# A two-pass graph network kernel: attention worked out by products inside pass 2, late edges scattered at the end, and pass 2's rows gathered as three bf16 parts

## The chip, the core and the metric

The kernel runs on one core of a Trainium2 chip. The metric is the device time of one execution in microseconds (us), the median of several runs. Beside it stands one profiled execution with a trace; the durations quoted come from that one.

## What is computed

There are 12500 nodes with 256 features each and 200000 edges (src, dst), sorted by dst. The reference is, cut to what matters:

```python
h = relu(layernorm(x))
h = h @ W_pre + b_pre
h = relu(gcn_conv(h, W1, b1)); h = relu(gcn_conv(h, W2, b2))   # with self loops, norm by degrees
x = x + h @ W_post + b_post
h = relu(layernorm(x))
xt = (h @ weight).reshape(N, 4, 64)
alpha = softmax(leaky_relu(alpha_l[src] + alpha_r[dst]), over the 4 heads)   # one row per edge
tmp[n] = sum over heads of alpha[n] * xt[dst[n]]        # n counts edges: edge n writes node n
x = x + tmp, repeated for the 4 heads
```

`alpha_l` and `alpha_r` are products of `xt` with small vectors, 4 numbers per node. The attention thus uses edges 0 to 12499 alone, edge n for node n. As the edges are sorted by dst, the dst of these lie in the first nine tiles of 128 nodes (XW = 9), while their src lie anywhere.

## The kernel before, in words

Nodes come in NT = 98 tiles of 128, edges in NCH = 112 chunks of 14 groups of 128 (the last chunk has 9 groups). The helper `convolve` (L1153) runs one convolution over all edges; it is called twice, as pass 1 and pass 2, with a table of rows in DRAM.

For each group t, POOL issues an indirect DMA (L1374) that gathers the 128 source rows into `fgot`, a ring of four buffers of one chunk each in pass 2. VectorE makes the one-hot matrices `fhot` of a whole chunk at once (L1241), and TensorE multiplies one-hot by rows into the sum `facc` in PSUM (L1382), which an fp32 matmul does in two records of the trace. At a chunk's end `close` lets ScalarE copy the sum (`fsums`, L1276), TensorE turn it (`fturn`, L1206, eight groups later) and VectorE add it to a sliding window `buf` (L1293, 13 groups later).

When a tile's window is complete, the steps of `finish1` (L1410) or `finish2` (L1464) are put into the list `due`, each with an offset in groups: `at` enters a step, `run` does all that are due, and `fills` names the PSUM tile that a step fills, so that a step that takes it over comes first. These offsets set the order of instructions on each engine; each engine runs its instructions in that order.

- `finish1`: product with W2's predecessor (L1417, +6), then ScalarE's relu into `fo` (L1422, +10), written to `table2` on the ACT queue.
- `finish2`: product with W2 (`fpz` L1472, +6), relu (`fy` L1479, `fz` L1482, +8), W_post (`fpo` L1488, +12), residual `fx` and its statistics, `kept_x` written on SP's queue (L1493 to L1501, +14), `h` on ScalarE (L1509, +16), its transpose (`fpt` L1514, +20; `ht` L1518, +22), the attention products (`fpx` L1527, +26), and at +28 a copy and small writes of `alpha_l` to `table_l` and `table_e` (L1535), of the first nine tiles' rows to `table_r`.

`prepare2` (L1454) loads what the next tile needs on SP's queue. Pass 2's first chunk is gathered by its own lists (`lacking`), so that it needs no row of pass 1's last two tiles; `late_sums` adds these by one-hots.

After pass 2 comes the attention stage (L1605 to L1711): for each group of seven tiles, POOL gathers `alpha_l[src]` per edge (`fal`, L1662); the rows of dst are built by one-hots `hot_t` (L1572) and products `fends` (L1652) out of `rows` (gathered by `own_rows`, L1577); products `lacks` (L1633) fill in src tiles that were not there at an earlier gather; VectorE does the softmax and the weighted sums `near`, `far`, `some`, `more`, `fmix`, `fres` (L1666 to L1694), and SP stores the group's 896 KB. The rows of 14 tiles are made inside pass 2 (L1553, for tiles 40 to 53).

If a check of the edge list fails, `bad_row` sends the execution to a general path, which is not part of the times here.

Of the kernel before, what the change touches and what calls it, by code (L numbers as in the profile page):

```python
# [413 lines left out]
def fast_path(  # L414
# [57 lines left out]
    table2 = dram.tile([NT * P, D], F32, name="ftable2")  # L472
    kept_x = dram.tile([NT * P, D], F32, name="kept_x")
# [3 lines left out]
    assert AC * J == NT and AC * CE <= E and XW < NT  # L477
    table_r = dram.tile([XW * P, DR], F32, name="table_r")
    table_l = dram.tile([NT * P, H], F32, name="table_l")

    LW = 3
    table_e = dram.tile([NT * P, H], F32, name="table_e")
# [18 lines left out]
    base_b = const.tile([P, NCH], F32, name="base_b")  # L501
    row_i = const.tile([P, AC], I32, name="row_i")
# [88 lines left out]
    with tc.tile_pool(name="fprep", bufs=1) as prep:  # L591
# [233 lines left out]
        with tc.tile_pool(name="fpsum", bufs=2, space=PSUM) as psum, \  # L825
# [227 lines left out]
            wide = prep.tile([NCH, P], F32, name="wide")  # L1053
            nc.vector.tensor_copy(wide, base.to_broadcast([NCH, P]))
# [7 lines left out]
            nc.tensor.matmul(fk[:, 2, :NCH], wide, ident[:NCH, :NCH], start=True, stop=True)  # L1062
# [7 lines left out]
            for f in after:  # L1070
                f()
            after = [raw_block(ends, m, psum.tile([P, 4 * P], F32, name="ft"), j0)
                     for j0 in (8, 12)]
            nc.vector.tensor_copy(base_b, fk[:, 2, :NCH])
            nc.vector.tensor_scalar(row_i, base_b[:, :AC], lane, float(XW * P - 1), op0=ALU.add,
                                    op1=ALU.min)
# [16 lines left out]
    def check_chunks(work, psum):  # L1093
# [20 lines left out]
        kept = work.tile([1, 1], F32, name="n_kept", bufs=1)  # L1114
        nc.vector.tensor_reduce(kept, pt[:1, 2, :NCH], AX.X, ALU.add)
        nc.vector.tensor_add(kept, kept, counted)
        nc.vector.tensor_scalar(bad_row, kept, -1.0, float(NCH + 1), op0=ALU.mult, op1=ALU.add)
# [12 lines left out]
    def load_late(pool):  # L1130

        nc.scalar.dma_start(roots, root_t)
        for t, w in ((wb, w2), (wo, w_post), (wg[:, :, :D], w_gat)):
            nc.scalar.dma_start(t, w.rearrange("(k p) n -> p k n", p=P))
        nc.scalar.dma_start(b2c, b2.rearrange("(k p) -> p k", p=P))
        nc.scalar.dma_start(bob, b_post.partition_broadcast(P))
        attn = []
        for a in (attn_r, attn_l):
            ar = pool.tile([P, D], F32, name="far", bufs=2)
            nc.scalar.dma_start(ar, a.rearrange("h c -> (h c)").partition_broadcast(P))  # L1140
            attn.append(ar)
        return attn

    def late_weights(pool, attn):

        for i, ar in enumerate(attn):
            for k in range(KC):
                prod = pool.tile([P, H, C], F32, name="fprod", bufs=1)
                nc.vector.tensor_mul(prod.rearrange("p h c -> p (h c)"), wg[:, k, :D], ar)
                nc.vector.tensor_reduce(wg[:, k, D + i * H:D + (i + 1) * H], prod, AX.X,  # L1150
                                        ALU.add)

    def convolve(ep, table, stride, width, ahead, with_sum, psum, prepare, finish, lacking=False,  # L1153
                 raw=(), rows_p=None):
# [28 lines left out]
        def run(now=None):  # L1183

            while due:
# [3 lines left out]
                do(d)  # L1189

# [41 lines left out]
        const_p = psum.tile([P, P if with_sum else P + D], F32, name="iota_p", bufs=1)  # L1232
        iota_p = const_p[:, :P]
        nc.vector.tensor_copy(iota_p, iota_w)
        if not with_sum:
            state["bias"] = const_p[:, P:]
            nc.vector.tensor_copy(state["bias"], bob)

# [4 lines left out]

        def hot_of(c):

            n = nj[c]
            h = ep.tile([P, J, P], F32, name="fhot", bufs=3)
# [3 lines left out]
        def new_rows_of():  # L1251
            if with_sum:
                return new_got()
            return rows_p.tile([P, J, stride], F32, name="fgot", bufs=ahead)

        def late_sums():

            h = ep.tile([P, J, P], F32, name="fhot", bufs=3)
# [5 lines left out]
            px = psum.tile([P, KC, P], F32, name="fpt", bufs=1)  # L1264
# [100 lines left out]
        for t, (c, j) in enumerate(tiles):  # L1365
# [7 lines left out]
            if c >= len(raw):  # L1373
                nc.gpsimd.indirect_dma_start(  # L1374
                    out=got, out_offset=None, in_=table[:(NT - TW) * P, :] if some else table[:],
# [4 lines left out]
            if j == (5 if some else 2) and c + 1 < NCH:  # L1380
                hots[c + 1] = hot_of(c + 1)
            nc.tensor.matmul(acc, hots[c][:, j, :], got[:, :width], start=(j == 0),  # L1382
                             stop=(j == nj[c] - 1 and not some))
# [6 lines left out]
            if c + 1 < len(raw):  # L1390
                raw_ahead(c + 1, j)
            run(t)
        run()
# [16 lines left out]
    def finish1(work, psum, w, buf, sbuf, fs):  # L1410
# [9 lines left out]
        def e():  # L1420
            o = work.tile([P, D], F32, name="fo", bufs=3)
            nc.scalar.activation(o, v["po"], AF.Relu, scale=dinv2[:, w:w + 1])  # L1422
            nc.scalar.dma_start(table2[w * P:(w + 1) * P, :], o)
            if w == 8:
                late_weights(late, attn)
                first_chunk()
            if w == 9:
                check_chunks(late, psum)

        return [(6, d, fills(w, "fpo")), (10, e, None)]  # L1430

    with tc.tile_pool(name="psum1", bufs=1, space=PSUM) as psum, \
# [6 lines left out]
                 rows_p=late)  # L1439
    ring.close()  # L1440

    ap = ctx.enter_context(tc.tile_pool(name="fatt", bufs=2))
    rows = [ap.tile([P, DR], F32, name="rows", bufs=AC) for c in range(AC)]
    EARLY = 2

    FROM = 40
    assert J % G == 0 and FROM > XW + 2 and FROM + J < NT - LW
    lates = {w: ap.tile([P, DA], F32, name="fxl", bufs=LW) for w in range(NT - LW, NT)}
    early = [ap.tile([P, G, DR], F32, name="fxe", bufs=J // G) for g in range(J // G)]
    hot_l = [ap.tile([P, CE], F32, name="hot_l", bufs=LW) for i in range(LW)]  # L1450

    def prepare2(work, w):  # L1454
# [6 lines left out]
        nc.sync.dma_start(xb[:n, :], x[w * P:w * P + n, :])  # L1461
        return rb, xb

    def finish2(work, psum, w, buf, pre, bias):  # L1464
        v = {"root": pre[0], "x": pre[1]}

        def d():
            pz = in_psum(psum, w, "fpz", [P, D], "facc", [P, D], 2)
# [16 lines left out]
        def f():  # L1485
            po = v["po"] = in_psum(psum, w, "fpo", [P, D], "facc", [P, D], 2)
# [4 lines left out]
        def g():  # L1491
# [9 lines left out]
            nc.scalar.activation(v["sc"], mv[:, 1:2], AF.Sqrt, bias=eps)  # L1501

# [8 lines left out]
        def i():  # L1511
            pt = v["pt2"] = in_psum(psum, w, "fpt", [P, KC, P], "fturn", [P, 2 * KC, P])
            for k in range(KC):
                nc.tensor.transpose(pt[:, k, :], v["h"][:, k * P:(k + 1) * P], ident)  # L1514

        def k():
            v["ht"] = work.tile([P, KC, P], F32, name="ht2")
            nc.scalar.activation(v["ht"], v["pt2"][:, :KC, :], AF.Copy)  # L1518
# [4 lines left out]
        def q():  # L1523
            px = in_psum(psum, w, "fpx", [P, DA], "iota_p", [P, P + D])
            px = v["px"] = px[:, d0:] if w + 1 < NT else px[:, :H]
# [4 lines left out]
        def r():  # L1530
            if w < NT - LW:
                xa = work.tile([P, DA], F32, name="fxa")
            else:
                xa = lates[w]
            nc.scalar.activation(xa[:, d0:], v["px"], AF.Copy)  # L1535
            nc.scalar.dma_start(table_l[w * P:(w + 1) * P, :], xa[:, DR:])
            if w < NT - LW:
                nc.scalar.dma_start(table_e[w * P:(w + 1) * P, :], xa[:, DR:])
            if w < XW:
                nc.scalar.dma_start(table_r[w * P:(w + 1) * P, :], xa[:, :DR])  # L1540

        steps = [(6, d, fills(w, "fpz")), (8, e, None), (12, f, fills(w, "fpo")), (14, g, None),
                 (16, h, None), (20, i, fills(w, "fpt")), (22, k, None),
                 (26, q, fills(w, "fpx")), (28, r, None)]
        t = w - FROM
        if 0 <= t < J:

            if t == 0:
                own_rows(0)

            def ends():
                px = v["ends"] = in_psum(psum, w, "fpx", [P, DA], None, None)[:, :DR]
                nc.tensor.matmul(px, hot_t[0][:, t * P:(t + 1) * P], rows[0], start=True,  # L1553
                                 stop=True)

            def copied():
                nc.scalar.activation(early[t // G][:, t % G, :], v["ends"], AF.Copy)

            steps += [(32, ends, "fpx"), (34, copied, None)]
        return steps  # L1560


    hot_t = {}

    def load_ends(pool, c, bufs):
        to_all = pool.tile([P, CE], I32, name="to_all", bufs=bufs)
        nc.sync.dma_start(to_all, dst[c * CE:(c + 1) * CE].partition_broadcast(P))
        return to_all

    def turn_hots(pool, c, to_all, bufs):  # L1570
        hot_t[c] = pool.tile([P, CE], F32, name="hot_t", bufs=bufs)
        nc.vector.tensor_scalar(hot_t[c], to_all, base_b[:, c:c + 1], lane,  # L1572
                                op0=ALU.subtract, op1=ALU.is_equal)

    def own_rows(c):

        nc.gpsimd.indirect_dma_start(  # L1577
            out=rows[c], out_offset=None, in_=table_r[:],
            in_offset=bass.IndirectOffsetOnAxis(ap=row_i[:, c:c + 1], axis=0))

    with tc.tile_pool(name="psum2", bufs=1, space=PSUM) as psum, \
            tc.tile_pool(name="fwork2", bufs=2) as work, \
            tc.tile_pool(name="edges2", bufs=1) as ep, \
            tc.tile_pool(name="fgots2", bufs=1) as rows_p:
        ep.tile([P, 320], F32, name="apart")
        for c in range(EARLY):
            turn_hots(ap, c, load_ends(work, c, 1), EARLY)
# [165 lines left out]
```

## Time and profile before

| | before |
|---|---|
| median of 9 runs | 4920.44 us (4892.04 to 4943.21) |
| the profiled execution | 4897.55 us |
| its span in the trace | 4895.7 us |
| granted TensorE clock, mean | 0.722 |
| pass 2, first to last gather issued | 2345.76 to 4634.98 us |
| last `fpx` | 4684.49 us |

How to read the views. In a line of the page's fifth part stand line, engine, operation, written tile and read tiles, how often, busy time in us, mean of one in ns, and the engine's idle time just before with what ended it. "issue" is time in which the engine waited for nothing that the profile shows; "remote" is a release by something that the profile does not name. A timeline line has start and length in us and, in brackets, the idle time before. Windows give each engine's busy time in a stretch of the span.

```profile
core 0: us, PE busy (x) PEld busy (x) DVE busy (x) ACT busy (x) POOL busy (x), PEclk, DMA share, GB/s
1000.00:1500.00 500.00, 287.57 (x978) 199.79 (x976) 79.59 (x138) 25.24 (x58) 330.84 (x351) 0.71 0.38 105
3000.00:3500.00 500.00, 267.33 (x1161) 226.52 (x1162) 112.55 (x240) 51.22 (x138) 319.46 (x338) 0.75 0.41 108
4640.00:4690.00 50.00, 34.32 (x169) 27.43 (x170) 18.96 (x60) 13.01 (x36) 5.45 (x6) 0.88 0.19 54
4690.00:4896.00 206.00, 82.27 (x245) 51.20 (x244) 107.96 (x202) 33.98 (x97) 91.48 (x96) 0.61 0.46 146
```

The four stretches lie in pass 1, in pass 2, at its end and in the attention stage.

### The profile page before, as it was taken

The page shows a single profiled execution, that of the slowest core. Times are in us where ns is not written, and L with a number is a line of the kernel's source. Part 1 is how long each engine was busy: PE and PEld are TensorE (multiplying, and loading weights), DVE is VectorE, ACT ScalarE, POOL GpSimd, SP SyncE. Part 2 cuts the span into 40 slices and gives each one's busy share as a digit, 9 for nine tenths or more (in the row PEclk, how much of TensorE's full clock was granted, in tenths as well). Part 3 has the DMA queues.
Part 4 walks back from the last instruction along what each step waited for, and adds up shares of the span by engine and source line. Part 5 has one row for each costly group of instructions (what it writes and reads, how often), then busy time and mean ns, then how long its engine had stood idle before and what let it go on. Part 6 is the DMA issues. An engine that isn't in the chain of part 4 may idle for free. (4 is left out here: it accounts for less than half of the span.)

```text
span 4895.7 us, 32267 instructions
## 1 busy us (share of the span) xinstructions
PE 2703.4 (55%) x10600; PEld 2070.1 (42%) x10600; DVE 1139.7 (23%) x2421; ACT 487.1 (10%) x1233; POOL 3103.0 (63%) x3299
## 2 busy tenths in 40 slices
PE   5655555555655655556445555454555555455553
PEld 4534433334434433434334444444444444444441
DVE  7412111111111111111222221222222222222236
ACT  5200000000000000000001110010111001100111
POOL 7566666666666666665566666666666666666633
PEclk7766767777766766676777777777777777777766
DMA  9433333333333333333334443443444444444434
GB/s 280 132 105 104 104 104 106 104 104 106 105 104 105 104 106 105 103 105 94 118 104 112 112 115 106 112 108 107 111 109 112 110 111 114 107 108 106 108 106 157
DMA packets 327419, 554.57 MB, mean 113 GB/s; under 512 B 96301, under 2 KB 224836, under 8 KB 327244
## 3 DMA queue, kind: packets, MB, share of 16 engines
q0 software_dynamic: 153520, 414.16, 31.4%
q1 hardware_dynamic: 127878, 121.99, 8.2%
q10 hardware_dynamic: 45846, 16.27, 1.3%
q8 instruction: 87, 1.43, 0.1%
q14 instruction: 88, 0.72, 0.0%
HBM read 498.89 MB, written 53.21 MB: 113 GB/s over the span
## 5 line engine op out<-in xcount | busy, mean ns | idle before, releaser
L1374 POOL DMA_INDIRECT fgot<-ftable,fsrc_t x3056 | 2892.0, 946 | 1564.6 <-issue 900.6
L1382 PE MATMUL facc<-fgot,fhot 128*128 128x257 f32 (+1 forms) x6252 | 1863.2, 439 | 625.5 <-issue 584.9
L1382 PEld LDWEIGHTS facc<-fgot,fhot 128*128 128x128 f32 x6252 | 1346.1, 223 | 981.4 <-issue 763.2
L1293 DVE TENSOR_TENSOR buf<-buf,fturn 128x256 f32 x224 | 94.3, 421 | 2034.6 <-remote 1265.0
L1241 DVE TENSOR_TENSOR fhot<-iota_p,to_t 128x1792 f32<-128x1792 f32 x224 | 448.8, 2004 | 13.4 <-PE fpt L1267 13.4
L1514 PE MATMUL fpt<-fident,h 128*128 128x128 f32 x194 | 60.3, 409 | 618.3 <-ACT h L1509 581.2
L1514 PEld LDWEIGHTS fpt<-fident,h 128*128 128x128 f32 x194 | 27.0, 189 | 658.1 <-ACT h L1509 616.7
L1417 PE MATMUL fpo<-wf,buf 128*128 128x256 f32 x388 | 132.3, 475 | 197.9 <-DVE buf L1293 153.8
L1479 DVE SCALAR_TENSOR_TENSOR fy<-rb,fb2c,fpz 128x128 f32<-128x128 f32 x194 | 58.7, 344 | 756.3 <-remote 320.6
L1488 PE MATMUL fpo<-fwo,fz 128*128 128x256 f32 x388 | 120.9, 439 | 204.6 <-ACT fz L1482 95.2
L1276 ACT ACTIVATE fsums<-facc 128x257 f32<-128x257 f32 (+1 forms) x224 | 85.4, 381 | 1403.7 <-remote 1183.0
L1493 DVE SCALAR_TENSOR_TENSOR fx<-fpo,fdinv,fxb 128x256 f32<-128x256 f32 x97 | 46.9, 484 | 693.9 <-remote 386.9
L1206 PE MATMUL fturn<-fident,fsums 128*128 128x128 f32 x448 | 109.8, 335 | 151.8 <-ACT fsums L1276 99.3
L1417 PEld LDWEIGHTS fpo<-wf,buf 128*128 128x128 f32 x388 | 91.5, 243 | 237.9 <-issue 183.1
L1472 PE MATMUL fpz<-buf,fwb 128*128 128x128 f32 x776 | 160.3, 376 | 19.4 <-DVE buf L1293 19.4
L1488 PEld LDWEIGHTS fpo<-fwo,fz 128*128 128x128 f32 x388 | 74.9, 212 | 219.8 <-ACT fz L1482 100.1
L1472 PEld LDWEIGHTS fpz<-buf,fwb 128*128 128x128 f32 x776 | 152.2, 289 | 23.9 <-DVE buf L1293 22.8
L1206 PEld LDWEIGHTS fturn<-fident,fsums 128*128 128x128 f32 x448 | 74.0, 175 | 208.1 <-ACT fsums L1276 117.3
L1422 ACT ACTIVATE fo<-fpo,fdinv 128x256 f32<-128x256 f32 x97 | 45.9, 473 | 953.7 <-remote 788.4
L1662 POOL DMA_INDIRECT fal<-table_l,fsrc_t x84 | 80.3, 957 | 74.2 <-DVE fs L1669 49.5
L1527 PE MATMUL fpx<-fwg,ht 128*128 128x4 f32 (+1 forms) x388 | 61.8, 268 | 115.9 <-issue 74.1
L1652 PE MATMUL fends<-rows,hot_t 128*128 128x260 f32 x168 | 71.5, 578 | 93.6 <-issue 63.6
(267 smaller groups left out, 1800.9 us busy)
## 6 DMA issues: line engine op xcount, KB each, us to landing
fgot<-ftable,fsrc_t POOLq DMA_INDIRECT x3056
self<-ftable SPq DMA_DIRECT2D x99, 128.0 KB
self<-ftable SPq DMA_DIRECT2D x97, 130.0 KB
ftable<-fo ACTq DMA_DIRECT2D x98, 128.0 KB
kept_x<-fx SPq DMA_DIRECT2D x98, 128.0 KB
fxb<-in_x_dram SPq DMA_DIRECT2D x97, 128.0 KB
fxr<-kept_x SPq DMA_DIRECT2D x13, 896.0 KB
out_dram<-fres SPq DMA_DIRECT2D x13, 896.0 KB
```

The lines of the kernel that those rows point to most:

```text
L1206: nc.tensor.transpose(v["pt"][:, i * KC + k, :], rows[:, k * P:(k + 1) * P], ident)
L1241: nc.vector.tensor_tensor(h, iota_p[:, None, :].to_broadcast([P, n, P]), to[:, :, None].to_broadcast([P, n, P]), ALU.is_equal)
L1276: nc.scalar.activation(sb, acc, AF.Copy)
L1293: nc.vector.tensor_add(b, b, v["pt"][:, :KC, :])
L1374: nc.gpsimd.indirect_dma_start(out=got, out_offset=None, in_=table[:(NT - TW) * P, :] if some else table[:], in_offset=bass.IndirectOffset ...
L1382: nc.tensor.matmul(acc, hots[c][:, j, :], got[:, :width], start=(j == 0), stop=(j == nj[c] - 1 and not some))
L1417: nc.tensor.matmul(po, buf[:, k, :P], wf[:, k, :], start=(k == 0), stop=False)
L1472: nc.tensor.matmul(pz[:, m, :], wb[:, k, m * P:(m + 1) * P], buf[:, k, :P], start=(k == 0), stop=(k == KC - 1))
L1488: nc.tensor.matmul(po, v["z"][:, m, :], wo[:, m, :], start=(m == 0), stop=(m == KC - 1))
L1514: nc.tensor.transpose(pt[:, k, :], v["h"][:, k * P:(k + 1) * P], ident)
L1652: nc.tensor.matmul(px, hot_t[c][:, j * P:(j + 1) * P], rows[c], start=True, stop=True)
L1662: nc.gpsimd.indirect_dma_start(out=al[:, i, :], out_offset=None, in_=(table_l if c else table_e)[:], in_offset=bass.IndirectOffsetOnAxis(a ...
```

## The change

**Rows of pass 2.** `finish1` keeps the relu in PSUM, copies it to a bf16 part and to `fo`, and a new step `split` (+12) makes the second and third bf16 part of what is left. SP writes the three parts (1536 bytes a row) to `parts2`. Pass 2 gathers these rows into three buffers instead of four, makes `fhot` in bf16, and multiplies three times per group:

```diff
+            v["parts"] = work.tile([P, 3, D], BF16, name="fparts", bufs=2)
+            nc.scalar.activation(v["parts"][:, 0, :], po, AF.Copy)
...
+        def split():
+            po, b = v["po"], v["parts"]
+            nc.vector.tensor_tensor(po, po, b[:, 0, :], ALU.subtract)
+            nc.vector.tensor_copy(b[:, 1, :], po)
+            nc.vector.tensor_tensor(b[:, 2, :], po, b[:, 1, :], ALU.subtract)
+            nc.sync.dma_start(parts2[w * P:(w + 1) * P, :], b.rearrange("p i d -> p (i d)"))
...
-            nc.tensor.matmul(acc, hots[c][:, j, :], got[:, :width], start=(j == 0),
-                             stop=(j == nj[c] - 1 and not some))
+            many = 1 if parts is None else 3
+            for i in range(many):
+                nc.tensor.matmul(acc, hots[c][:, j, :], got[:, i * width:(i + 1) * width],
+                                 start=(j == 0 and i == 0),
+                                 stop=(j == nj[c] - 1 and i == many - 1 and not some))
```

**Work in between.** `convolve` gets a list `behind`. `feed(t)` takes its first item when the item's condition holds, spreads its parts over the next groups, and takes the next item after a given number of groups. After the last group `at_end` is called.

```diff
+        def feed(t):
+
+            if behind and t >= free_at[0] and behind[0][0]():
+                _, space, parts = behind.pop(0)
+                for i, part in enumerate(parts):
+                    if part:
+                        at(t + i, lambda _, part=part: part())
+                free_at[0] = t + space
```

**The list of late edges.** In pass 1, once 11 tiles are done, `list_late` lists the edges whose src lies in tile 84 (LATE) or later, in up to 16 columns of 128. It has 62 parts, one every second group: small operations, transposes, 98 bf16 products and a few small DMAs, and more checks that add to `bad_row`.

**Attention in pass 2.** `alpha_l` of every tile stays in SBUF (`l_all`). `attend` gives these items, with the groups that each occupies: 98 loads of table rows by SP at an address read from SBUF (`ends_of_tile`, 1 each), 14 `alpha_r` (4), 4 `late_hots` (6), 16 `late_ends` (4), 14 x 4 `alpha_l` for src tiles 0 to 71 (4), and from tile 84 on 14 `group` (8), each with the last `alpha_l` stage (tiles 72 to 83), the softmax, weights, the mix and, for tiles below 84, the load of `kept_x` and the store of the output. Three `rest` items do this for the other tiles. One `alpha_l`:

```diff
+            def equal():
+                v["h"] = hot_of(v["row"], "lane")
+
+            def product():
+                v["p"] = bank()[:, :G * nw * H].rearrange("p (t w h) -> p t w h", t=G, h=H)
+                for j in range(G):
+                    nc.tensor.matmul(v["p"][:, j, :, :], v["h"][:, j * P:(j + 1) * P],
+                                     l_all[:, w0:w1, :], start=True, stop=True)
+
+            def taken():
...
+                nc.vector.tensor_tensor(v["p"], v["p"],
+                                        mask[:, :, :, None].to_broadcast([P, G, nw, H]), ALU.mult)
+                some = ap.tile([P, G, H], F32, name="some_l", bufs=1)
+                nc.vector.tensor_reduce(some, v["p"].rearrange("p t w h -> p t h w"), AX.X,
+                                        ALU.add)
+                nc.vector.tensor_add(al[:, t, :], al[:, t, :], some)
+
+            return [load, None, equal, product, taken]
```

To make room in PSUM, `finish2` uses two shared banks, `fX` for `fpz` and `fpo` and `fY` for `fpt` and `fpx`; two banks are called `behind`.

**The end.** The old attention stage, `table_l`, `table_e`, `own_rows`, `hot_t` and the early ends are gone. `tail_begins` (called as `at_end`) loads `late_hot` and `late_end` into the `fgot` buffers and fetches 11 of 16 columns of `kept_x` with POOL; in `prepare2` the last tile's own loads are issued in front of these loads. After pass 2 come the other five fetches, 16 products, the softmax of the late edges, their mix, and 16 indirect scatters by POOL into the output:

```diff
+        for k in range(KL):
+            nc.tensor.matmul(z[k // 8][:, k % 8, :, :], sets["hot"][:, k * P:(k + 1) * P],
+                             l_all[:, LATE:, :], start=True, stop=True)
...
+            for i in range(k0, k0 + n):
+                nc.gpsimd.indirect_dma_start(
+                    out=out[:], out_offset=bass.IndirectOffsetOnAxis(ap=late_i[:, 0, i:i + 1],
+                                                                     axis=0),
+                    in_=sets["x"][:, i, :], in_offset=None)
```

## The prediction

> **What bounds the kernel now.** I began with the page's busy times and its costliest groups.
>
> ```profile
> PE 2703.4 (55%) x10600; PEld 2070.1 (42%) x10600; DVE 1139.7 (23%) x2421; ACT 487.1 (10%) x1233; POOL 3103.0 (63%) x3299
> ...
> L1374 POOL DMA_INDIRECT fgot<-ftable,fsrc_t x3056 | 2892.0, 946 | 1564.6 <-issue 900.6
> L1382 PE MATMUL facc<-fgot,fhot 128*128 128x257 f32 (+1 forms) x6252 | 1863.2, 439 | 625.5 <-issue 584.9
> ```
>
> No engine is full, and the largest is POOL, which issues the gathers: 946 ns each, and then idle time whose larger half is "issue". The view of POOL's waits splits that idle time (sum, times, longest).
>
> ```profile
> POOL fgot L1374 <- issue: 904.5, 2907, 11.7
> POOL fgot L1374 <- remote: 525.5, 140, 7.4
> POOL fgot L1374 <- PE facc L1382: 129.4, 15, 10.8
> ```
>
> So a gather costs 0.946 + 0.30 = 1.25 us while POOL runs on, and some 155 times POOL stops for a buffer that PE has not given back. To see the rhythm I read the timelines of POOL, PE and ACT around 3400 us, in pass 2.
>
> ```profile
> 3398.57 0.94 POOL L1374 DMA_INDIRECT fgot<-ftable,fsrc_t  x1 [2.92 <-remote]
> ...
> 3414.81 0.95 POOL L1374 DMA_INDIRECT fgot<-ftable,fsrc_t  x1 [0.30 <-issue]
> 3418.62 0.94 POOL L1374 DMA_INDIRECT fgot<-ftable,fsrc_t  x1 [2.86 <-remote]
> ```
>
> ```profile
> 3407.48 3.62 PE L1382 MATMUL facc<-fgot,fhot 128*128 128x256 f32 x16
> 3419.30 0.69 PE L1514 MATMUL fpt<-fident,h 128*128 128x128 f32 x2 [8.21 <-ACT h L1509]
> ```
>
> ```profile
> 3418.38 0.38 ACT L1276 ACTIVATE fsums<-facc 128x256 f32<-128x256 f32 x1 [8.34 <-remote]
> 3418.66 0.59 ACT L1509 ACTIVATE h<-fx,nb,sc 128x256 f32<-128x256 f32 x1
> ```
>
> POOL issues 14 gathers (one chunk) in 17.5 us, stops some 2.6 us, and goes on: 20.1 us a chunk. PE has done its work of the chunk by 3411.1, but ACT sees the chunk's sum ready only at 3418.38, after POOL's last gather ended (3415.76). PE then waits 8.21 us for `h`, which stands behind that sum on ACT. So what PE reports late in a run of gathers reaches the others only once POOL is quiet, and POOL itself waits for such a report. In pass 1 the stops are 5.2 us after runs of 28: again 0.186 us a gather, though pass 1 does less on PE per tile. I read 1.25 + 0.186 = 1.436 us per gather as the price of the passes, not set by PE's work; why reports are late the trace does not say. Two passes of 1563 gathers fill nearly all of 4896 us. The rest that matters is the end, which the view of the chain shows from 4660 us on.
>
> ```profile
> 4684.49 0.68 PE fpx L1527 x4
> 4685.40 1.36 DMA table_l<-fxl
> ...
> 4727.42 5.89 another core or an unknown queue
> ...
> 4738.62 4.49 another core or an unknown queue
> ...
> 4746.21 8.77 PE lacks L1633 x42
> ```
>
> The last tile's attention row is done at 4685.2; the span ends at 4895.7. This stage of 211 us is attention alone, and steps between PE and ACT there cost 4.4 to 5.9 us while POOL fetches `fal`.
>
> **The end, removed and rebuilt.** All 211 us of it go. Left after the last `fpx` is the late edges' work. Rows of the stage itself give the prices:
>
> ```profile
> L1633 PE MATMUL lacks<-fxl,hot_l 128*128 128x4 f32 x84 | 15.2, 318 | 0.0
> ...
> L1685 DVE TENSOR_TENSOR near<-fxg,share 128x896 f32<-128x896 f32 x11 | 11.9, 1086 | 0.4
> ...
> L1690 DVE TENSOR_TENSOR more<-near,far 128x448 f32<-128x448 f32 x13 | 8.1, 623 | 0.0
> ```
>
> - copy of the last `px` into `l_all`: 0.4.
> - 16 score products, two records each as every fp32 product here: 32 x 15.2/84 = 5.8.
> - mask and sum of 448 elements, twice each: 4 x 0.62 = 2.5.
> - softmax: seven small operations of 0.18 to 0.23 and two handovers to ACT: 2.5.
> - near, mix, add of the first two columns (512 elements each): 3 x 0.67 = 2.0.
> - 16 scatters on POOL at 1.25, as its gathers: 20. DVE makes four columns in some 3.6 us and POOL needs 5 for them, so DVE hides.
> - landing 2.45 us as gathers show, and the end 1.5.
>
> Sum 37, with 4 for waits 41: **-170**. The loads of `late_hot` and `late_end` (3.1 MB) start when pass 2's last gather buffers come free, some 12 us before that point; at the 157 GB/s of the page's last slice they take 20, and so could add 8. Eleven of the 16 `kept_x` fetches lie beside PE's last tiles, five wait for the last tile (6 us, beside the score products). Bounds: -180 with no wait, -120 if loads, `rest` stores and scatters follow each other.
>
> **Pass 1.** finish1 gets two ACT copies (0.4 each) and three DVE operations (0.42 as `buf`), 2 us a tile on engines that are 5% and 16% busy from 1000 to 1500 us; POOL's stops hide it. `list_late` spreads 62 parts over 124 steps, nine chunks. Each may lengthen a wait by a stop: 0 to 9 x 5.2 = 47; I take **+10**, as nothing there stands on POOL. The split also comes between the last tile and pass 2, whose first gather now waits for the write of `parts2`: 3 x 0.42 + more bytes, **+3**, beside a 37.1 us wait of before.
>
> **Pass 2's rows in bf16.** POOL's issue: 128 rows per gather as before. Gathers of 16-byte rows took 957 ns and of 1024-byte rows 946, so I take 1536 bytes at no cost; if time went by bytes, these rows would show it. The queue's share (31.4% of the DMA engines) would grow by up to a half, still not full. On PE a product of 256 columns in fp32 is two records at 426 ns, 852; three in bf16 by the nearest row (L567, 256 columns, 272 ns) are 816. That is 36 ns a gather, 56 us of the pass if PE set it, and nothing by the 1.436 above: **0**, bounds -200 (see the second rival) to +60, the latter if three instructions instead of two are late where reports are late. Three buffers instead of four shorten POOL's lead by 20 us; since each stop waits for one buffer per chunk, I take 0.
>
> The Trainium skill, page "TensorE: Matmul & The Clock Gate", section "HAM oscillation", says that waits of PE longer than some 3.4 us drop it to half clock. It speaks against thinning PE's work: PE waits 8.21 us per chunk already (granted clock 0.75 from 3000 to 3500 us), and bf16 would make this longer. By its section "Back-to-back issue gap" (N/2.4 ns warm, N/1.2 cold) I estimate 42 products of a chunk at 4.6 us warm and 9.0 cold; 28 records at 3.62/16 are 6.3 today. By the rule the chunk could lose 2.7 us to a colder clock; by the trace's slack of 8 us it loses nothing.
>
> **Attention inside pass 2.** Steps that hold attention work: 14 `alpha_r` x 4, 4 `late_hots` x 6, 16 `late_ends` x 4, 56 `alpha_l` x 4, 14 groups x 8 = 480 gathers, 34 of 112 chunks. One `alpha_l` adds on DVE a one-hot of 896 (1.09, as `near`), mask and product and sum of 126, 504 and 504 (0.2 + 0.65 + 0.65) and a small add (0.18): 2.8 us. On PE it adds 7 products, 14 records at 0.181: 2.5. Per chunk 3.5 of these: DVE 9.8 on top of 4.6 (112.55 of 500 us), PE 8.8 on top of some 11. Both fit into 20.1 us as sums. What may not fit is the order: `taken` waits for PE, the next one-hot and the next chunk's `fhot` stand behind it on DVE, and PE waits for those. After the tenth microsecond of a run PE's report is late, so about one item in a chunk sits out the rest of the run, and its work comes after POOL stopped. I price that as one more stop like those of today, 2.6 us per chunk: 34 x 2.6 = **+88**. Bounds: 0 (all in the quiet time) and 34 x 8.21 = 279 (one more wait like that for `h`). The 98 loads of table rows with an address read by SP lie in 7 chunks more; SP's other loads are issued a tile ahead (23 us): **+5**, bounds 0 to 50. Gone are two small DMA issues per tile on ACT (0.33 + 0.44) and the early ends of 14 tiles, all hidden today: 0.
>
> **Sum** on the profiled execution (4897.55, span 4895.7): -170 + 10 + 3 + 88 + 5 = -64, 4833.6. The median of the runs, 4920.44, is 22.9 above the profiled one: forecast **4856** (-1.3%). A measurement of this kernel can tell about 0.5%, 25 us, from no change.
>
> **Rivals.**
> 1. *Slower: attention's round trips price by the step, not by the chunk.* Place: the 34 chunks. 14 + 56 items with one report of PE to DVE each and 14 groups with five make 140; at half of the 4.9 us that such a step cost in the old end, 343 instead of 88: **5111**. For it: those rows of 4.49 and 5.89. Against it: when PE is late POOL stops by itself, and reports pass then. It decides from (170 - 18)/34 = 4.5 us per chunk.
> 2. *Faster: PE's lighter product ends the stops.* If PE's chunk end comes before the reports turn late, POOL does not stop in the 78 light chunks, 78 x 2.6 = 203, and the heavy ones lose nothing: **4565**. For it: PE's chunk end lies just at the edge. Against it: equal price per gather in both passes.
> 3. *The end is not as short as it says:* loads, late stores and scatters in a row, -120 instead of -170: **4906**, no change.
>
> **How the numbers follow.** Forecast 0.45 (own range 4800 to 4920), first rival 0.30, second 0.13, third 0.12. Half of the outer rivals' cases lie beyond their times, so 4565 to 5111 leaves out some 0.21; the range is 4560 to 5115. Faster by over 0.5% (below 4896): 0.45 x 0.85 + 0.13 + 0.02 = 0.53; within: 0.06 + 0.08 = 0.14; slower: 0.30 + 0.03 = 0.33.
>
> **What would show it.** Right: POOL's stops in light chunks still 2.6 us per 14 gathers; heavy chunks at 22 to 23 us; last `fpx` near 4790 and some 41 us behind it, 16 scatters 1.25 apart. Wrong: heavy chunks beyond 24.6 us with DVE `taken` waiting on PE (first rival), chunks of 17.5 us in a row (second), POOL's gathers longer than 946 ns with 1536-byte rows, or first gather of `parts2` much later than 37 us.

## The result, and the profile after

The changed kernel takes 5139.12 us (median of 14 runs, 5122.15 to 5152.19) beside 4920.15 us for the kernel before (46 runs). The ratio is 1.0442, 95% interval 1.0422 to 1.0461: slower by 4.4%. The profiled execution took 5129.23 us, its span is 5127.4 us.

First the page of the changed kernel, busy times and costliest groups.

```profile
PE 2934.0 (57%) x13647; PEld 2202.7 (43%) x13647; DVE 1489.0 (29%) x3189; ACT 551.9 (11%) x1429; POOL 3034.6 (59%) x3226
...
L1411 PE MATMUL facc<-fgot,fhot 128*128 128x256 bf16 (+1 forms) x7815 | 1830.9, 379 | 802.4 <-issue 764.8
L1400 POOL DMA_INDIRECT fgot<-parts,fsrc_t x1549 | 1465.4, 946 | 1150.7 <-PE facc L1411 509.1
L1400 POOL DMA_INDIRECT fgot<-ftable,fsrc_t x1507 | 1425.9, 946 | 776.1 <-issue 443.9
```

A gather of 1536-byte rows (`parts`) takes POOL 946 ns like one of pass 1. New is what POOL waits for in pass 2: 509.1 us for `facc` on PE. The view of POOL's waits (sum, times, longest) puts it beside the 15 waits and 129.4 us of before:

```profile
POOL fgot L1400 <- issue: 896.8, 2886, 7.3
POOL fgot L1400 <- PE facc L1411: 564.3, 47, 21.4
POOL fgot L1400 <- remote: 447.3, 117, 5.7
```

Where the 231.7 us of the two spans come from, by the starts of the first and last gathers:

| stretch | before | after | difference |
|---|---|---|---|
| up to the last gather of pass 1 | 2307.7 | 2326.3 | +18.6 |
| from there to pass 2's first gather | 38.0 | 36.9 | -1.1 |
| pass 2, first to last gather | 2289.2 | 2632.3 | **+343.1** |
| last gather to the end | 260.7 | 131.8 | **-128.9** |

The end got shorter as the change wanted it, by 41 us less than I thought; pass 2 lost 343 where I had allowed 93. Pass 2's loss stands in few places. These are the times from the first gather of a chunk to that of the next (POOL's timeline), changed kernel:

```
chunks  52 to  58 (no attention):   20.3 20.3 19.4 20.8 20.2 20.3 20.3
chunks  23 to  27 (alpha_r):        27.3 27.6 27.9 29.7 27.9
chunks  47 to  51 (alpha_l):        21.6 33.9 27.0 34.2 20.3
chunks 102 to 109 (groups):         34.3 37.6 31.7 38.6 36.5 38.5 33.0 38.2
```

Chunks without attention take 20.3 us beside 20.1 before, although their products are in bf16. Below, the **loss** of a kind of item is the sum, over its chunks, of what exceeds 20.1 us: alpha_r (chunks 23 to 28) 40, late_ends (29 to 34) 27, the four alpha_l stages (35 to 38, 47 to 51, 67 to 72, 87 to 93) 158, groups (102 to 110) 126. In the kernel before the same chunks give 0, 2, 13 and 6, from its pairs of 17.5 and 28 us. How far these sums vary by themselves shows the last run below, `aside`, with the same pass 2: 47, 30, 163 and 134, and 2657 us for pass 2 instead of 2632.

One alpha_r chunk shows how it comes about. First POOL, then PE, in the timeline of the changed kernel.

```profile
2897.34 0.94 POOL L1400 DMA_INDIRECT fgot<-parts,fsrc_t  x1 [10.35 <-PE facc L1411]
...
2913.57 0.95 POOL L1400 DMA_INDIRECT fgot<-parts,fsrc_t  x1 [0.30 <-issue]
2925.24 0.94 POOL L1400 DMA_INDIRECT fgot<-parts,fsrc_t  x1 [10.72 <-PE facc L1411]
```

```profile
2902.27 1.70 PE L1962 MATMUL behind<-right,hot_s 128*128 128x4 f32 x14
...
2905.88 0.49 PE L1411 MATMUL facc<-fgot,fhot 128*128 128x256 bf16 x3 [0.47 <-DMA fgot<-parts,fsrc_t]
2909.51 0.79 PE L1962 MATMUL behind<-right,hot_s 128*128 128x4 f32 x3 [3.14 <-issue]
2910.87 0.17 PE L1962 MATMUL behind<-right,hot_s 128*128 128x4 f32 x1 [0.57 <-issue]
2912.96 0.59 PE L1962 MATMUL behind<-right,hot_s 128*128 128x4 f32 x3 [1.92 <-issue]
2915.78 0.90 PE L1962 MATMUL behind<-right,hot_s 128*128 128x4 f32 x4 [2.23 <-issue]
2917.22 0.80 PE L1962 MATMUL behind<-right,hot_s 128*128 128x4 f32 x3 [0.54 <-issue]
2917.88 1.44 PE L1411 MATMUL facc<-fgot,fhot 128*128 128x256 bf16 x6
```

POOL issues 14 gathers without a break, the last ends at 2914.5. For nine microseconds PE runs as it should: 14 records of an item take 1.70 us. From 2906 on the next 14 such records take 12 us, a few at a time, with idle time that the profile calls "issue". At 2917.9, 3.4 us after POOL stopped, PE is quick again, but the rest of the chunk is still to be done, and POOL waits for it until 2925.24. Before the change PE was through with its chunk 12.5 us into POOL's run (3411.1 in the prediction's lines, after a start at 3398.57); now work is left over, and it is done while POOL stands still.

### The profile page after: what moved, and what is told of

Same layout as the page of the kernel before. It is cut to its first block, busy times and chain, and to the rows that moved or that the text cites. A ratio compares the mean times of both kernels' runs of the same rounds, so it can differ in the third digit from the quotient of the medians.

```text
span 5127.4 us, 39554 instructions
## 1 busy us (share of the span) xinstructions
PE 2934.0 (57%) x13647; PEld 2202.7 (43%) x13647; DVE 1489.0 (29%) x3189; ACT 551.9 (11%) x1429; POOL 3034.6 (59%) x3226
## 5 line engine op out<-in xcount | busy, mean ns | idle before, releaser
L1411 PE MATMUL facc<-fgot,fhot 128*128 128x256 bf16 (+1 forms) x7815 | 1830.9, 379 | 802.4 <-issue 764.8
L1400 POOL DMA_INDIRECT fgot<-parts,fsrc_t x1549 | 1465.4, 946 | 1150.7 <-PE facc L1411 509.1
L1400 POOL DMA_INDIRECT fgot<-ftable,fsrc_t x1507 | 1425.9, 946 | 776.1 <-issue 443.9
L1411 PEld LDWEIGHTS facc<-fgot,fhot 128*128 128x128 f32 x3126 | 686.8, 227 | 653.8 <-issue 537.8
L1411 PEld LDWEIGHTS <-fhot 128*128 128x128 bf16 x4689 | 546.6, 119 | 595.3 <-issue 470.2
L1263 DVE TENSOR_TENSOR fhot<-iota_p,to_t 128x1792 f32<-128x1792 f32 (+1 forms) x224 | 448.9, 2004 | 12.1 <-remote 12.1
L1983 PE MATMUL behind<-l_all,hot_s 128*128 128x72 f32 (+1 forms) x980 | 174.1, 349 | 138.3 <-DVE hot_s L1882 95.8
L1983 PEld LDWEIGHTS behind<-l_all,hot_s 128*128 128x128 f32 x980 | 166.6, 263 | 156.8 <-issue 144.4
L1764 PE MATMUL fX<-buf,fwb 128*128 128x128 f32 x776 | 156.6, 365 | 13.2 <-issue 13.0
L1764 PEld LDWEIGHTS fX<-buf,fwb 128*128 128x128 f32 x776 | 146.5, 279 | 13.9 <-issue 13.4
```

What stands on the lines that cost most here:

```text
L1263: nc.vector.tensor_tensor(h, iota_p[:, None, :].to_broadcast([P, n, P]), to[:, :, None].to_broadcast([P, n, P]), ALU.is_equal)
L1400: nc.gpsimd.indirect_dma_start(out=got, out_offset=None, in_=rows_of[:(NT - TW) * P, :] if some else rows_of[:], in_offset=bass.IndirectOf ...
L1411: nc.tensor.matmul(acc, hots[c][:, j, :], got[:, i * width:(i + 1) * width], start=(j == 0 and i == 0), stop=(j == nj[c] - 1 and i == many ...
L1764: nc.tensor.matmul(pz[:, m, :], wb[:, k, m * P:(m + 1) * P], buf[:, k, :P], start=(k == 0), stop=(k == KC - 1))
L1983: nc.tensor.matmul(v["p"][:, j, :, :], v["h"][:, j * P:(j + 1) * P], l_all[:, w0:w1, :], start=True, stop=True)
```

## The experiments

Two theories to begin with. **Window:** PE advances and reports well only in some ten microseconds after POOL restarts, and while POOL issues nothing; what an attention item leaves over at the end of that window is done with POOL stopped. **Price by the step:** each item costs its products and round trips wherever it stands. A time without a ratio is that of one execution, the others are medians of four or more.

**Fewer items per chunk.**

```diff
-            items.append((when("w", XW), 4, alpha_r(b)))
+            items.append((when("w", XW), 8, alpha_r(b)))
```

The same 4 became 8 for `late_ends` and `alpha_l`.

> The attention is complete; alpha_r, late_ends and alpha_l items start every 8 gathers instead of every 4, so a chunk holds 1.75 of them instead of 3.5, over twice as many chunks. Against light chunks of 20.3 us the changed kernel loses in pass 2: alpha_r 38.9, late_ends 25.4, alpha_l 33 to 50 in each of four stages (152), groups 126. Window theory (what PE must still do when its first ten microseconds after POOL's restart are over is done with POOL stopped): half as many items fit nearly into the window, so these 216 us fall below 90, the kernel gets 120 us or more faster. Price by the step (each item costs its round trip wherever it stands): the 216 us stay within 30, only spread over more chunks at half the excess each.

Measured 5033.44 us, ratio to the kernel before 1.0214 (1.0189 to 1.0238); pass 2 2568 us. Chunks 23 to 101, which hold all items but the groups, lose 191 instead of 248. Neither expectation holds: spreading helps, but far less than the window asked for. My reading, which no run shows, is that light chunks fill most of the window themselves, so half as many items still leave something over.

**Breaks in POOL's issue.**

```diff
+        calm = None if parts is None else work.tile([P, 1024], F32, name="calm", bufs=1)
...
+            if parts is not None and j in (6, 13):
+                nc.gpsimd.memset(calm, 0.0)
```

So POOL clears a scratch tile after every seventh gather.

> After every seventh gather of pass 2 POOL clears a scratch tile (128 x 1024 numbers, an estimated 1 us), so no run of gathers is longer than seven. The computation is complete. Window theory: reports pass in each pause, light chunks keep about 20.3 us because the pause takes the place of a stop, and the excess of the attention chunks (343 us more in pass 2 than before) falls by a third or more: 100 us faster or better. Price by PE's and VectorE's work: the added 224 clears cost what they take, 200 us slower, attention chunks unchanged.

Measured 5001.05 us, ratio 1.0158 (1.0131 to 1.0185). Pass 2 takes 2531 us, 101 less, though POOL does 216 us more work in it (223 clears of 970 ns). Light chunks are 19.2 and 21.0 in turn, some 20.1: the clears take the place of stops. This speaks for the window. By item: alpha_r 28, late_ends 16, alpha_l 136, groups 106.

**PE's share and the waits' share of one item.**

```diff
-                v["h"] = hot_of(v["row"], "lane")
+                pass
...
-                    nc.tensor.matmul(v["p"][:, j, :, :], v["h"][:, j * P:(j + 1) * P],
+                    nc.tensor.matmul(v["p"][:, j, :, :], ident,
...
```

The rest of the edit empties `taken`: VectorE's mask, product and sum are left out too.

> alpha_l keeps its loads and its seven products, but with a constant matrix as weights, and VectorE's work of it is left out (one-hot, mask, product, sum): the scores of src are missing, the output is not the reference's. No step of alpha_l waits for another engine. Theory of PE's work (leftover products): the four alpha_l stages keep most of their 152 us of excess, over 100. Theory of round trips (PE waits for one-hots that wait for VectorE's taking the last product): below 50.

Measured 4984.47 us; the alpha_l stages lose 87 instead of 158.

```diff
-                for j in range(G):
-                    nc.tensor.matmul(v["p"][:, j, :, :], v["h"][:, j * P:(j + 1) * P],
-                                     l_all[:, w0:w1, :], start=True, stop=True)
+                n = G * nw * H
+                nc.tensor.matmul(v["p"].rearrange("p t w h -> p (t w h)"), v["h"][:, :P],
+                                 ends.rearrange("p t c -> p (t c)")[:, :n], start=True, stop=True)
```

> alpha_l keeps VectorE's work and both waits between PE and VectorE, but has one product of the same output width instead of seven (its output is not the reference's). Theory of PE's work: the excess of the alpha_l stages falls from 152 to below 75 us. Theory of round trips: it stays above 110.

Measured 4992.84 us; the stages lose 87 as well. Both results lie between the two expectations. Neither the products alone nor the waits alone are the price: taking either away wins some 71 of the 158 us, and together that is nearly all. This fits the window, which does not care what fills it; a price by the step made up of both halves would fit as well, so these two runs do not decide.

**All of attention out of pass 2.** The four kinds of items `ends_of_tile`, `alpha_r`, `alpha_l` and `group` are not put into the list.

> The loads of table rows, alpha_r, alpha_l and the groups are left out of pass 2 (the output of nodes below tile 84 is not written, that of late edges is not the reference's); rows in bf16, three buffers, the list of late edges and the whole end stay. If attention alone is what pass 2 lost: every chunk at 20.1 to 20.3 us, pass 2 from first to last gather 2250 to 2290 us instead of 2632, the whole 4780 +-25. If three bf16 products or three buffers cost something of their own: chunks above 20.5. If the lighter product frees POOL: chunks below 20.0.

Measured 4822.99 us; pass 2 takes 2323 us, with light chunks of 20.3 and, as before the change, some pairs of 17.5 and 27.8. So attention alone accounts for 309 of the 343 us. The forecast of 2290 was missed by 33, of which `late_ends`, still there and now in chunks 19 to 22, takes 23; the lighter product freed nothing.

**Undoing bf16.**

```diff
-            return rows_p.tile([P, J, 3 * stride], BF16, name="fgot", bufs=ahead)
+            return rows_p.tile([P, J, 320], F32, name="fgot", bufs=ahead)
...
-                 parts=parts2)
```

> The changed kernel with pass 2's rows gathered in fp32 from the old table (three buffers, one fp32 product per gather, fp32 one-hots; the parts are still written, but not read). The computation is complete. If bf16 saves PE work that the attention chunks lack: their loss grows from 343 by 40 us or more (42 records instead of 28, but shorter ones), light chunks stay at 20.3. If bf16 does nothing: pass 2 within 20 us of 2632. If three short products hurt: pass 2 shorter by 30 us or more.

Measured 5153.62 us, pass 2 2660 us. That is 28 above the changed kernel, but 3 above the same pass 2 in `aside`; alpha_l loses 169 beside 158 and 163. So these runs show no gain from the bf16 rows, and not the 40 us or more by which fp32 rows should have been slower.

**More breaks where attention stands.**

```diff
+            if parts is not None and (j % 3 == 2 if any(a <= c <= b for a, b in (
+                    (23, 37), (47, 51), (67, 72), (87, 93), (102, 110))) else j in (6, 13)):
+                nc.gpsimd.memset(calm, 0.0)
```

> As with the clear after every seventh gather (5001 us, pass 2 2531), but in the attention chunks a clear (0.97 us) after every third gather, four per chunk. The computation is complete. Window theory: PE's reports pass within 4 us of POOL's issue, alpha_r and alpha_l chunks fall to POOL's 17.5 + 3.9 = 21.4 us plus little, the excess of alpha_l from 136 to below 90 and of the groups from 106 to below 90: 4930 +-20. If the items' own length along PE and VectorE sets these chunks: within 15 us of 5001.

Measured **4865.47 us**, ratio to the kernel before 0.9871 (0.9806 to 0.9936): 274 us below the changed kernel, better than expected. All items are in it. POOL's timeline in one alpha_r chunk, and PE's in the next:

```profile
2909.09 0.95 POOL L1401 DMA_INDIRECT fgot<-parts,fsrc_t  x1 [0.17 <-issue]
2910.35 0.95 POOL L1401 DMA_INDIRECT fgot<-parts,fsrc_t  x1 [0.30 <-issue]
2911.61 0.95 POOL L1401 DMA_INDIRECT fgot<-parts,fsrc_t  x1 [0.30 <-issue]
2912.55 0.97 POOL L1407 MEMSET calm<- 128x1024 f32 x1
2913.68 0.95 POOL L1401 DMA_INDIRECT fgot<-parts,fsrc_t  x1 [0.17 <-issue]
...
2916.94 0.94 POOL L1401 DMA_INDIRECT fgot<-parts,fsrc_t  x1 [1.06 <-PE facc L1414]
```

```profile
2923.32 1.68 PE L1965 MATMUL behind<-right,hot_s 128*128 128x4 f32 x14
...
2926.61 1.62 PE L1965 MATMUL behind<-right,hot_s 128*128 128x4 f32 x14
...
2930.71 1.62 PE L1965 MATMUL behind<-right,hot_s 128*128 128x4 f32 x14
```

Three gathers, a clear, three gathers: PE's items now take 1.6 to 1.7 us throughout a chunk. The records that PE starts per microsecond, by the time since a chunk's first gather and averaged over the chunks of a kind, from the two traces:

| us since the first gather | 0-4 | 4-8 | 8-12 | 12-16 | 16-20 |
|---|---|---|---|---|---|
| alpha_r, changed kernel | 4.6 | 4.4 | 2.0 | 2.2 | 1.7 |
| alpha_r, with these breaks | 3.7 | 3.7 | 4.6 | 6.5 | 5.8 |
| alpha_l, changed kernel | 2.9 | 5.1 | 4.8 | 2.5 | 0.9 |
| alpha_l, with these breaks | 4.1 | 4.7 | 3.9 | 5.3 | 5.1 |
| groups (102 to 109), changed kernel | 3.1 | 3.1 | 3.9 | 3.6 | 2.5 |
| groups (102 to 109), with these breaks | 3.1 | 3.3 | 4.2 | 4.8 | 5.5 |

So the window is no fixed ten microseconds: in alpha_r chunks PE falls off after eight, in alpha_l chunks after twelve, and in the groups hardly at all before POOL's run ends. What PE idles there is mostly "issue": 0.45 of the time from 8 to 20 us in alpha_r chunks and 0.42 from 12 to 20 us in alpha_l chunks, with the breaks 0.07 and 0.06. Why the moment differs no run shows.

Most chunks with alpha_r, late_ends and alpha_l stand at 20.8 us, which is POOL's own time for 14 gathers and four clears. Losses: alpha_r 6, late_ends 4, alpha_l 34, groups 76; pass 2 2381 us.

**The same clears in one place.** Is it the breaks, or only the slower pace of gathers?

```diff
-            if parts is not None and (j % 3 == 2 if any(
+            if parts is not None and (j == 13 if any(
...
```

Four clears stand behind the 14th gather of such a chunk.

> As with the clear after every third gather of the attention chunks (4865 us, pass 2 2381), but the four clears of such a chunk stand together behind its 14th gather: POOL issues as many gathers and clears per chunk, in one run of 17.5 us instead of runs of 3.75. The computation is complete. If unbroken issue keeps PE from advancing: the attention chunks lose most of what they lost in the changed kernel again, pass 2 above 2530, the time above 5000. If only the lower pace of gathers counts: pass 2 within 30 us of 2381.

Measured 5054.22 us, ratio 1.0280 (1.0247 to 1.0313); pass 2 2602 us; alpha_r 32, late_ends 27, alpha_l 159, groups 137. The view of POOL's waits, of this kernel and then of the one with breaks:

```profile
POOL fgot L1401 <- PE facc L1415: 357.9, 40, 21.6
```

```profile
POOL fgot L1401 <- PE facc L1414: 164.3, 31, 14.0
```

With as many gathers and clears per chunk, unbroken issue brings the loss back, as the window said. It is the length of the unbroken run. Whether the issuing itself counts, or the transfers that it sets going, these runs do not separate.

**Do clears and spreading win the same time?** `late_ends`, `alpha_r` and `alpha_l` every 8 gathers, groups every 11, a clear after every seventh gather.

> Complete: alpha_r, late_ends and alpha_l every 8 gathers, groups every 11, and a clear after every seventh gather. Spreading gave 105 us and the clears 138. If they win from different waits they add to some 4920, level with the kernel before; if both free the same waits, 4970 to 5000.

Measured 4928.61 us, ratio 0.9995 (0.9968 to 1.0021), close to the 4920 of the first case. In chunks 23 to 101 the loss is 79; it was 248 in the changed kernel, 191 with spreading alone and 182 with the clears alone. So they do not win the same time: together they won more than the sum. The groups, 8 apart in both single runs, lose 97 here.

**Groups further apart, with breaks.**

> As with the clear after every third gather of the attention chunks (4865 us), with the groups 11 gathers apart instead of 8, so that a chunk holds 1.3 of them instead of 1.75. The computation is complete. There the group chunks still took 28 to 34 us and lost 76 us while every other attention chunk stood at POOL's 20.8. If a group chunk is now bound by PE's own work (a fixed price per group), the loss stays within 15 us of 76 and the time within 20 us of 4865; if it was too little room per chunk, the loss falls below 45 and the time to 4830 or below.

The clears of every third gather stand in chunks 101 to 111 here instead of 102 to 110. Measured **4844.99 us**, ratio 0.9825 (0.9784 to 0.9865), the lowest median of all; groups lose 40 instead of 76 in chunks 102 to 110. That speaks for room per chunk, but the time missed the 4830 expected: pass 2 is 41 us shorter, and 24 of them come back behind its last gather (142 us to the end instead of 118).

**Clears in the kernel before.** The tiles `rows[3:]`, unused until pass 2 is over, are cleared after every seventh gather.

> The kernel before with a clear of about a microsecond (four tiles of 260 numbers) on POOL after every seventh gather of pass 2, all else unchanged and complete. If the clears only take the place of stops that POOL would make anyway: chunks stay at 20.1 us on average and the time is within 25 us of the kernel before, perhaps 20 to 35 faster where chunks of 28 us go. If clears help every chunk: 100 us faster or more; then the gain of the clears is not due to attention. If they cost their own time: 200 us slower.

A break is four clears of 0.33 us here. Measured 4873.36 us, ratio 0.9889 (0.9859 to 0.9918), 60 us below the kernel before on the same chip and more than the 20 to 35 expected. In the trace pass 2 takes 2256 us instead of 2289: a chunk takes 20.1 on average instead of 20.4, and those of 28 us are gone. Where the rest of the 60 us lies the traces do not say. So a part of the gain of the clears is to be had without the change. With clears in both, on the same chip, the changed kernel (4844.99) is 28 us ahead of the kernel before, though the latter has fewer breaks.

**The scatters at the end.**

```diff
-                    out=out[:], out_offset=bass.IndirectOffsetOnAxis(ap=late_i[:, 0, i:i + 1],
+                    out=aside[i][:N, :], out_offset=bass.IndirectOffsetOnAxis(ap=late_i[:, 0, i:i + 1],
```

> Each of the 16 scatters at the end writes into a scratch tensor of its own instead of the output (the late edges' rows of the output are missing), so that no scatter has to wait for the landing of the one before. In the changed kernel they start 2.7 to 3.4 us apart, 44 us in all. Expected if that wait alone keeps them apart: 1.25 us apart, 19 us, 25 us less from the last score to the end. If the form of the scatter keeps them apart: unchanged.

POOL's timeline of the changed kernel, then of this one:

```profile
5073.39 0.97 POOL L2200 DMA_INDIRECT out_dram<-fgot,late_i  x1 [2.61 <-DMA out_dram<-fgot,late_i]
5076.60 0.97 POOL L2200 DMA_INDIRECT out_dram<-fgot,late_i  x1 [2.24 <-DVE tail_near L2192]
5079.28 0.97 POOL L2200 DMA_INDIRECT out_dram<-fgot,late_i  x1 [1.71 <-DMA out_dram<-fgot,late_i]
```

```profile
5095.83 0.98 POOL L2201 DMA_INDIRECT aside<-fgot,late_i  x1 [0.31 <-issue]
5097.11 0.97 POOL L2201 DMA_INDIRECT aside<-fgot,late_i  x1 [0.30 <-issue]
```

The first to the last scatter take 19.7 us instead of 44.3, and the stretch from the last gather to the end 105 instead of 132. As expected, a scatter into the output waits for the landing of the one before. The time (5129.20) does not differ, as pass 2 happened to take 2657 here.

## Why the prediction was wrong

**The step that failed** is the price of attention inside pass 2: "I price that as one more stop like those of today, 2.6 us per chunk: 34 x 2.6 = +88", with an upper bound of 8.21 a chunk, 279. Measured: 343 in pass 2, where POOL's stops are 10 to 12.5 us in chunks of alpha_r and 14 to 21 in those of the groups. The sum of the parts was -64; measured on the spans is +232, and pass 2 makes 250 of the 296 between them. Two misreadings stand behind it.

*Chunks of alpha_r, late_ends and alpha_l, 225 us of loss.* I had read that reports are late after the tenth microsecond of a run, and that what is behind comes after POOL stopped, but counted only the delay of the reports. PE itself hardly advances in that time, as the 14 records in 12 us show, so all that an item leaves over is added. Breaks in POOL's issue took this loss to 45 us.

*Groups, 126 us of loss.* Here "Both fit into 20.1 us as sums" was wrong. That sum took every heavy chunk to hold 3.5 items like one `alpha_l`, 8.8 us of PE. A group holds more products, and their busy time in chunks 102 to 108 (12 groups) is:

```profile
L1411 PE MATMUL facc<-fgot,fhot 128*128 128x256 bf16 x288 | 69.5, 400 | 4.2 <-issue 4.2
...
L2040 PE MATMUL behind<-turned_a,pick 28*128 28x128 f32 x163 | 39.2, 404 | 6.1 <-ACT turned_a L2034 6.1
L1983 PE MATMUL behind<-l_all,hot_s 128*128 128x48 f32 x168 | 35.4, 389 | 22.0 <-DVE hot_s L1882 20.7 <-DVE sc L1797 1.1 <-issue 0.2
...
L2055 PE MATMUL behind<-ends_all,weights 128*128 128x64 f32 x154 | 33.0, 403 | 2.1 <-issue 2.1
...
L2029 PE MATMUL behind<-fident,al_all 128*28 128x128 f32 x12 | 4.4, 368 | 21.7 <-DVE al_all L1847 11.6 <-DVE m_all L1845 5.8 <-DVE sc L1797 4.2
```

The last four lines are the groups' own, 112 us or 16 a chunk. In all, PE was busy for 233.6 of the 288.4 us of chunks 102 to 109, 29.2 a chunk, more than the 20.1 that POOL needs; before it was 11.1 a chunk. The "issue" idle time that marks the other chunks is 0.9 us a chunk here, beside 6.7 in those of alpha_r. So it is mainly PE's own work that sets the pace there; with the breaks it was 24.9 us a chunk. The upper bound of 8.21 a chunk was too low for it (126 over nine chunks are 14). The range's end, 5115, came from the first rival's 5111.

**Clock.** The clock goes into that work.

```profile
3000.00:3500.00 500.00, 295.96 (x1624) 232.07 (x1624) 162.80 (x332) 52.13 (x148) 273.28 (x291) 0.70 0.52 151
4750.00:4820.00 70.00, 60.50 (x273) 50.47 (x271) 32.84 (x71) 11.32 (x23) 26.46 (x28) 0.52 0.61 187
```

These windows of the changed kernel have the granted clock in the third column from the right. In the groups PE is busy for 60.5 of 70 us at a clock of 0.52, and 14 records of 48 columns take 3.2 us in some items and 1.8 in others. My sums had used a mean record of 0.181 us. With a clear after every third gather the same products (1068 records instead of 1060 in chunks 102 to 109) kept PE busy for 199.4 us at a clock of 0.65. An estimate: busy time times clock is 126 us with 233.6 x 0.54, and 130 with 199.4 x 0.65, so the 34 us that PE saved there go with the clock. What set the clock is not shown. The rule of the Trainium skill that I weighed ("TensorE: Matmul & The Clock Gate", section "HAM oscillation", a wait of PE of over some 3.4 us halves the clock) fits these traces only in part: chunks 102 to 109 have seven waits of PE over 3.4 us at a clock of 0.54, and two at 0.65 with the breaks, but the kernel before has eight in the same chunks at 0.75, and chunks 52 to 61 of the changed kernel nine at 0.71.

**The first rival** had 5111, within 0.6% of the result, and the same 343 for pass 2. Its reason, a price by the step wherever it stands, does not hold: with every step in place, breaks in POOL's issue took the loss of alpha_r from 40 to 6 and of alpha_l from 158 to 34. That its number fits is chance.

**The second rival** is refuted: chunks without attention stay at 20.3 us with bf16 rows. The product was hardly lighter either. I had taken 272 ns for a bf16 record, 816 for three; the mean in pass 2 is 330, and with the overlap of records PE is busy with them for 7.6 us a chunk beside 8.3 in fp32 before. That 1536-byte rows cost POOL nothing was right (946 ns), and so was that some 1.44 us a gather is not set by PE's work while that work fits (20.3 us per 14 gathers in light chunks, and in the kernel without items).

**The end** was priced at -170. Of the steps after the last `fpx` (5056.5) the products took 7.1 instead of 5.8, and the first scatter started 13.3 us behind it, as summed. Mis-sized were the scatters, 44 instead of 20, as the price of a gather left out the wait of one write for another, and what follows the last scatter's start, 13.3 instead of 4. Together 70.9 instead of 41. What fills the 13.3 us behind the last scatter's start the trace does not say. Ahead of the last `fpx` 11 more us went, from the last gather to it 61 instead of 50; POOL's 11 fetches of `kept_x` lie there, but I did not test that. So the third rival had a part of the truth: the scatters stand in a row, and the end's 129 us are nearer to its 120 than to 170.

**Pass 1** has +18.6 against +10. The other kernels with this very pass 1 took 2161 to 2200 us from its first to its last gather (five of them 2161 to 2170, the other six 2194 to 2200), the kernel before 2178, the changed one 2194, so that number is within their spread. For the same reason differences in the whole time between these kernels can hold some 30 us that no edit made; those of pass 2 are the safer ones. The 98 loads by SP (5 us) were not tested by themselves; chunks 17 to 22, in which most of them lie, lost 9.

## What to carry to other kernels

Where one engine issues gathers without a break, look at the others' records late in such a run, before putting work there: slack as a sum over a chunk is no slack, if it lies in the time in which an engine does not advance. Price added work by what it leaves over when the good stretch ends, and add up each kind of item by itself: one kind may fit into a chunk and another not. A short operation that keeps the issuing engine from issuing, every few gathers, can be worth more than it costs; and scatters into one tensor are priced by their landing, not by their issue.

## What was unexpected of the hardware

- In chunks with unbroken gathers by POOL, TensorE falls from 4 to 5 records started per microsecond to between 0.9 and 2.5, after eight us of the run (alpha_r) or twelve (alpha_l), and is idle with no wait that the profile shows for over 0.4 of that time. In the chunk shown it is quick again 3.4 us after the last gather. Breaks of 0.97 us after every third gather keep the pace up; the same clears in one place behind the 14th do not. Why issue on POOL holds up TensorE no run here shows. The Trainium skill says ("DMA: Bandwidth & Descriptors", section "SWDGE vs HWDGE vs iDMA") that the descriptors of such gathers are written by GpSimd into rings in SBUF; whether TensorE meets these writes no run here shows.
- 216 us of clears on POOL made pass 2 101 us shorter, and in light chunks cost nothing (19.2 and 21.0 us in turn instead of 20.3).
